# A four-layer graph network on one core: a selection matrix formed by transposes on PE, and table rows of 528 numbers

## The chip, the core and the metric

The kernel runs on one core of a Trainium2 chip. The metric is the device time of one execution in microseconds (us). PE is the matrix engine (PEld its weight loads), DVE the vector engine, ACT the scalar engine, POOL the general engine GpSimd, which here also issues the gathers, and SP the engine that issues the plain DMAs.

## The reference, cut to what matters

Eight batches of 2048 nodes with 64 features go through four layers over one sparse graph `adj`. Each layer normalizes its input, clamps it at zero, attends over a node's neighbours, and adds the result to its input.

```python
# layer 0: scores are dot products
h = jnp.maximum(_layernorm(x, axis=-1), 0.0)
x = x + _L0_gnn_ref(h, adj)
# layer 1: e[n,m] = leaky(s1[n] + s2[m]), then ELU
h = jnp.maximum(_layernorm(x, axis=-1), 0.0)
x = x + _L1_gnn_ref(h, adj, L1_gnn_W, L1_gnn_a)
# layer 2: four heads of dot products, a projection, then a second
# attention by dot products, then a layer norm
h = jnp.maximum(_layernorm(x, axis=-1), 0.0)
x = x + _L2_gnn_ref(h, adj, L2_gnn_Wh, ..., L2_gnn_beta)
# layer 3: like layer 1, with relu
h = jnp.maximum(_layernorm(x, axis=-1), 0.0)
x = x + _L3_gnn_ref(h, adj, L3_gnn_W, L3_gnn_a)
```

In the additive layers 1 and 3 a node needs of each neighbour its feature row (8 batches x 64 = 512 numbers) and the second term of its score, one number for each batch.

## The kernel before

**Tiles.** `edge_stack` cuts the 2048 nodes into 16 tiles of 128, one node for each partition, with all eight batches side by side (F = 512 numbers, B = 8 batches). Of the dense graph it makes lists of neighbours once. Tile i has `ROWS[i]` slots in which every node has one neighbour of its own, and `PACKED[i]` slots in which 128 further edges of any of the tile's nodes are packed: 81 slots in all, 32 of them packed (`sum(PACKED)`).

**Selection matrices.** For a packed slot, a 128x128 matrix of zeros and ones says which node an edge belongs to. `sel(i, t)` carries a node's value to its edges (`by_edge`, L406, and the query product in `scores`, L428); its transpose `selt(i, t)` sums edges back into their nodes (`by_query`, L392, and `weigh_sum`, L385). Both are made while the lists are made: `sel` by comparisons (L670), `selt` from it by transposes on PE and copies on ACT (L671 to L677). `selt_all` stays in the on-chip memory (SBUF) to the end. `sel_all[0]` lies in the pool `rows` (L582), which ends with layer 1; a copy of 2 MB goes to DRAM at L709, and is loaded back at L857, at the start of the stage after the heads.

**Stages.** In the order of the source: making of the lists and the first normalization; layer 0; layer 1 (`additive(1, ...)`, L710); the four heads of layer 2 (L714 to L849, pools `l2`, `ps_z`, `ps_s`, `ps_g`); the second attention of layer 2 (L852 to L902; the prediction calls it layer 3's start, after its table number 3); and the last layer (`additive(4, ...)`, L909, table 4; the prediction's layer 4). Each stage writes its rows to a table in DRAM (`store_rows`, L352), and the next gathers from it: one indirect DMA of 128 rows for each slot, issued by POOL (`gather`, L246), into a ring of 26 slots in SBUF (L100). So the first gather of a stage waits for the last row of the stage before.

**Tables.** Tables 1 and 4, of the two additive layers, have rows of F + B = 520 numbers: 512 features and, behind them, the 8 second terms, which `pre_d` copies there (L348). The others have 512. The ring has rows of 520 for all. The second terms are read as `g[:, :, F:]` (L507, L532, L535).

**Order.** Within a stage `pipeline` (L214) writes the tiles' steps in a skewed order: while one tile is gathered, the one before is scored, the one before that is weighted. In the second attention these are `take3` (gathers and the load of the tile's own rows), `first3` (squares L866, products L422 and L430, weights L436), `second3` (sums of weights, then `weigh_sum`: POOL multiplies rows by weights at L380, PE sums them at L385), `third3` and `fourth3`. That is not yet the order of the engines: the program is built with a planner that simulates the instructions' times and sorts each engine's queue by them:

```python
with tile.TileContext(nc, schedule_with_timeline_sim=True) as tc:
```

Buffers of a closed pool are handed on to the next one. The pools of the stage after the heads, where `sel` is to lie, and its sums in PSUM, are:

```python
with psum_pools()[0] as ps_q, psum_pools()[1] as ps_t, tc.tile_pool(name="rows2", bufs=2) as rp:
    ...
    sel_all[0] = rp.tile([P, sum(PACKED) * P], F32, name="sel", bufs=1)
    nc.sync.dma_start(out=sel_all[0], in_=sel_dram[:, :])
```

`ps_q` has three banks of 512 numbers.

Of the kernel before, what the change touches and what calls it, by code (L numbers as in the profile page):

```python
# [8 lines left out]
F32 = mybir.dt.float32  # L9
# [3 lines left out]
AF = mybir.ActivationFunctionType  # L13
OP = mybir.AluOpType
AX = mybir.AxisListType

P = 128
# [42 lines left out]
def edge_stack(ctx: ExitStack, tc: tile.TileContext, x_in, adj, w1, w1t, a1, wh, wht, bh, wo, bo,  # L60
# [9 lines left out]
    nc = tc.nc  # L70
    N, F = x_in.shape
    D = gamma.shape[0]
    B = F // D
# [22 lines left out]
    f1s = const.tile([P, NT, B], F32, name="f1s")  # L96
    over = const.tile([P, NT, 3], F32, name="over")
    most = const.tile([P, 5, NT], F32, name="most")
    least = const.tile([P, 2, NT], F32, name="least")
    ring = const.tile([P, RING, F + B], F32, name="g")  # L100
    qidx = const.tile([P, sum(PACKED)], I32, name="qidx")
    selt_all = const.tile([P, sum(PACKED), P], F32, name="selt")
# [3 lines left out]

    table = [tc.dram_tile([N + 2, F + B if k in (1, 4) else F], F32, name=f"table{k}")
             for k in range(5)]

    QW = B * H * D + B * H  # L110
    qtab = tc.dram_tile([N + 2, QW], F32, name="qtab")
    sel_dram = tc.dram_tile([P, sum(PACKED) * P], F32, name="seld")
    xs = [tc.dram_tile([P, F], F32, name=f"xs{i}") for i in range(NT)]
# [13 lines left out]
    nc.gpsimd.memset(zcol, 0.0)  # L127
    zrow = const.tile([1, F + B], F32, name="zrow")
    nc.gpsimd.memset(zrow[:, :F], 0.0)
# [104 lines left out]
    def rows(i, lo, hi, most=RING):  # L234

        t = lo
        while t < hi:
# [3 lines left out]
            t += m  # L241

    def row(i, t):
        return ring[:, (held[i] + t) % RING, :F]
# [68 lines left out]
    def pre_c(u):  # L313
        def f(i, st):
            st["xh"] = rows_pool[0].tile([P, F + B], F32, name="xh", bufs=3)
# [22 lines left out]
    def pre_d(k, u):  # L338

        def f(i, st):  # L340
            xh = st["xh"]
            if u is not None:
                p = ps_m.tile([P, F], F32, name="m")
                for j in range(F // P):
                    nc.tensor.matmul(p[:, 4 * j:4 * j + 4], st["xt"][:, j, :], u, start=True, stop=True)
                pv = p[:, :2 * B].rearrange("p (b t) -> p t b", t=2)
                nc.scalar.copy(f1s[:, i, :], pv[:, 0, :])
                nc.scalar.copy(xh[:, F:], pv[:, 1, :])  # L348
            store_rows(k, i, xh, k != 2)
        return f  # L350

    def store_rows(k, i, xh, mean):  # L352
        cols = table[k].shape[1]
        nc.sync.dma_start(out=table[k][i * P:(i + 1) * P, :], in_=xh[:, :cols])
        if mean:
            if i == order[0]:
                nc.gpsimd.tensor_copy(acc, xh[:, :F])
            else:
                nc.gpsimd.tensor_tensor(acc, acc, xh[:, :F], op=OP.add)
            if i == order[-1]:  # L360
                p = ps_m.tile([P, F], F32, name="m")
                nc.tensor.matmul(p[:1, :], ones, acc, start=True, stop=True)
                mr = rows_pool[0].tile([1, F + B], F32, name="mr", bufs=1)
                nc.vector.memset(mr[:, F:], 0.0)
                nc.vector.tensor_copy(mr[:, :F], p[:1, :])
                nc.sync.dma_start(out=table[k][N:N + 1, :], in_=mr[:, :cols])
# [133 lines left out]
    def additive(k, wd, *finish):  # L500
# [21 lines left out]
        def first(i, st):  # L522
# [57 lines left out]
    with tc.tile_pool(name="rows", bufs=2) as rp:  # L580
# [133 lines left out]
    with tc.tile_pool(name="l2", bufs=2) as l2p, \  # L714
# [116 lines left out]
        def fourth2(i, st):  # L831
# [9 lines left out]
            for b in range(4):  # L841
                nc.tensor.transpose(p[:, b * P:(b + 1) * P], ht[:, b * P:(b + 1) * P], ident)
            h2 = rows_pool[0].tile([P, F + B], F32, name="xh", bufs=3)
            nc.scalar.copy(h2[:, :F].rearrange("p (j b d) -> p b j d", j=2, d=D),
# [7 lines left out]
    with psum_pools()[0] as ps_q, psum_pools()[1] as ps_t, tc.tile_pool(name="rows2", bufs=2) as rp:  # L852
# [3 lines left out]
        sel_all[0] = rp.tile([P, sum(PACKED) * P], F32, name="sel", bufs=1)  # L856
        nc.sync.dma_start(out=sel_all[0], in_=sel_dram[:, :])  # L857

# [581 lines left out]
```

## Time and profile before

| what | value |
|---|---|
| median of three runs | 1717.97 us (1717.35 to 1723.83) |
| the profiled execution | 1721.51 us, span 1719.7 us |
| DMA in all | 266.94 MB in 85787 packets |
| of it gathers (POOL's queue) | 141.05 MB |
| plain DMAs (SP's queue) | 124.79 MB |
| gathers `g<-table,idx` | 405, POOL busy 986 ns with each |
| store and load of the selection matrix | 1 each, 2048 KB |

The stages by the profile's table of stretches (busy us of each engine, and share of the DMA engines in use):

| stretch, us | PE | DVE | ACT | POOL | DMA |
|---|---|---|---|---|---|
| 110 to 365, lists and layer 0 | 168.9 | 243.3 | 81.0 | 189.3 | 0.54 |
| 365 to 655, layer 1 | 214.4 | 202.7 | 157.2 | 132.6 | 0.54 |
| 655 to 1195, the heads | 470.2 | 430.5 | 258.4 | 459.1 | 0.45 |
| 1195 to 1262, passage to the second attention | 34.3 | 26.1 | 18.6 | 31.9 | 0.56 |
| 1262 to 1530, second attention | 185.5 | 227.6 | 135.1 | 196.1 | 0.34 |
| 1530 to 1720, last layer | 135.7 | 102.7 | 17.9 | 75.9 | 0.50 |

Times in the text are from the span's start. A line of the chain of waits reads: start, duration, then the engine or DMA that the end of the program was waiting on at that time. In a line of waits, "DVE mr L364 <- DMA table<-xh: 5.6, 1, 5.6" means that DVE, before the instruction of line 364 that writes `mr`, waited 5.6 us in all, once, 5.6 at most, and that the landing of that DMA ended the wait. "issue" is waiting that the profile explains by nothing, "remote" waiting ended by an event that it can't place.

### The profile page before, as it was taken

The numbers are of one execution on the slowest core, as the hardware profiler recorded it, in microseconds if no ns is written. First come the engines' busy times: TensorE is split into PE (matmuls) and PEld (weight loads), VectorE is DVE, ScalarE is ACT, GpSimd is POOL, SyncE is SP. The second block draws the span as 40 slices with busy tenths as digits, with TensorE's granted clock in tenths as the row PEclk, the third lists the DMA queues.
The fourth block names the chain that finished last, engine by engine and source line by source line (L and its number), as shares of the span: only waits on it lengthen the run. The fifth ranks groups of instructions, "written<-read, shape, count | busy, mean of one in ns | idle before, by whom it ended". The sixth has DMA issues, their size and how long they took to land.

```text
span 1719.7 us, 15784 instructions
## 1 busy us (share of the span) xinstructions
PE 1215.1 (71%) x3771; PEld 606.6 (35%) x3771; DVE 1318.4 (77%) x2748; ACT 744.5 (43%) x2378; POOL 1153.4 (67%) x903
## 2 busy tenths in 40 slices
PE   0025667776479974599997999999467877555877
PEld 0002334443234431234342444443223433333545
DVE  6979999992469987699997899831389889823656
ACT  5841324441146783356531545545234445620011
POOL 5766867786554125898789889985577896654540
PEclk9998876896699997799999999999787879657989
DMA  5555454455566447656255345200643542235651
GB/s 172 167 182 179 152 200 153 141 198 156 147 201 235 158 179 260 233 189 208 87 201 200 113 157 177 87 13 19 255 141 99 154 146 70 81 119 164 197 170 51
DMA packets 85787, 266.94 MB, mean 155 GB/s; under 512 B 14627, under 2 KB 14659, under 8 KB 75446
## 3 DMA queue, kind: packets, MB, share of 16 engines
q0 software_dynamic: 37328, 141.05, 26.7%
q1 hardware_dynamic: 48358, 124.79, 20.4%
q8 instruction: 32, 0.52, 0.1%
q14 instruction: 69, 0.57, 0.1%
HBM read 208.74 MB, written 57.05 MB: 155 GB/s over the span
## 4 chain that ended last, share of the span: by engine, by line
PE 25%; POOL 11%; DVE 9%; issue 7%; ACT 5%; DMA 3%; another core or an unknown queue 2%; DVEq 0%; SPq 0%; POOLq 0%; ACTq 0%
PE y L787 10%; PE y L385 4%; POOL g L253 3%; POOL wh L772 3%; PE m L836 2%; ACT yn L795 2%; PE m L824 2%; PE y L779 2%; POOL wg L380 1%; DMA g<-table,idx 1%; POOL ln_r L290 1%; DMA rows<-table 1%; PE m L399 1%; DVE prod L755 1%
## 5 line engine op out<-in xcount | busy, mean ns | idle before, releaser
L253 POOL DMA_INDIRECT g<-table,idx x405 | 399.2, 986 | 233.5 <-issue 161.7
L772 POOL TENSOR_TENSOR wh<-g,w 128x1024 f32<-128x1024 f32 x162 | 307.5, 1918 | 30.0 <-PE y L787 28.0
L385 PE MATMUL y<-wg,ident 128*128 128x512 f32 x392 | 234.5, 729 | 72.7 <-POOL wg L380 64.3
L290 POOL TENSOR_TENSOR ln_r<-ln_q,mhalf 128x8 f32<-128x8 f32 x80 | 135.8, 1701 | 160.6 <-DVE ln_q L288 85.1
L759 DVE TENSOR_REDUCE s<-prod 128x32 f32<-128x2048 f32 x81 | 184.0, 2286 | 14.8 <-ACT w L761 12.9
L380 POOL TENSOR_TENSOR wg<-g,w 128x1024 f32<-128x1024 f32 (+1 forms) x91 | 158.9, 1756 | 37.3 <-ACT w L436 24.2
L787 PE MATMUL y<-wh,ident 128*128 128x512 f32 x320 | 154.6, 610 | 28.9 <-POOL wh L785 25.1
L385 PE MATMUL y<-wg,selt 128*128 128x512 f32 x256 | 141.6, 663 | 5.4 <-POOL wg L380 4.4
L385 PEld LDWEIGHTS y<-wg,ident 128*128 128x128 f32 x392 | 81.6, 228 | 162.2 <-POOL wg L380 78.9
L787 PE MATMUL y<-wh,selt 128*128 128x512 f32 x256 | 124.7, 614 | 10.4 <-POOL wh L772 10.4
L795 ACT ACTIVATE yn<-y,rec 128x64 f32<-128x64 f32 x512 | 111.2, 368 | 27.5 <-PE y L787 26.9
L755 DVE TENSOR_TENSOR prod<-q,g 128x2048 f32<-128x2048 f32 x49 | 111.5, 2276 | 5.3 <-ACT g L753 4.6
L399 PE MATMUL m<-w,selt 128*128 128x8 f32 (+1 forms) x384 | 59.5, 258 | 76.0 <-ACT w L542 38.2
L380 DVE TENSOR_TENSOR wg<-g,tiny 128x1024 f32<-128x1024 f32 (+1 forms) x92 | 98.2, 1086 | 17.1 <-PE y L385 8.8
L399 PEld LDWEIGHTS m<-w,selt 128*128 128x128 f32 x384 | 63.5, 213 | 122.3 <-ACT w L542 43.6
L442 DVE SCALAR_TENSOR_TENSOR zt<-m,bhc,att 128x512 f32<-128x512 f32 x64 | 47.3, 738 | 75.0 <-ACT att L441 74.4
L298 ACT ACTIVATE xh<-x,ln_r 128x64 f32<-128x64 f32 x256 | 88.3, 428 | 18.8 <-POOL ln_r L292 18.7
L787 PEld LDWEIGHTS y<-wh,ident 128*128 128x128 f32 x320 | 59.0, 193 | 104.9 <-issue 63.8
L428 PE MATMUL q<-rows,sel 128*128 128x512 f32 x128 | 84.3, 762 | 15.7 <-DVE prod L422 5.0
L753 ACT COPY g<-g 128x512 f32<-128x512 f32 x81 | 50.4, 622 | 100.5 <-DVE prod L755 87.9
L755 DVE TENSOR_TENSOR prod<-qe,g 128x2048 f32<-128x2048 f32 x32 | 73.0, 2282 | 17.0 <-DMA qe<-qtab,qidx 15.9
L779 PE MATMUL y<-rows,ident 128*128 128x512 f32 x128 | 70.0, 634 | 18.3 <-DMA rows<-table 13.6
(210 smaller groups left out, 2584.7 us busy)
## 6 DMA issues: line engine op xcount, KB each, us to landing
qtab<-q SPq DMA_DIRECT2D x16, 1040.0 KB
a<-in_adj_dram SPq DMA_DIRECT2D x16, 1024.0 KB
q<-qtab SPq DMA_DIRECT2D x14, 1040.0 KB
table<-xh SPq DMA_DIRECT2D x48, 256.0 KB
rows<-table SPq DMA_DIRECT2D x48, 256.0 KB
xs<-x SPq DMA_DIRECT2D x48, 256.0 KB
x<-xs SPq DMA_DIRECT2D x48, 256.0 KB
table<-xh SPq DMA_DIRECT2D x32, 260.0 KB
```

Of the source, the lines that this page charges most:

```text
L253: nc.gpsimd.indirect_dma_start(out=ring[:, (held[i] + t) % RING, :cols], out_offset=None, in_=table[k][:, :], in_offset=bass.IndirectOffse ...
L290: nc.gpsimd.tensor_tensor(st["rstd"][:, 0, :], q, mhalf, op=OP.pow)
L298: nc.scalar.activation(dst[:, b * D:(b + 1) * D], st["src"][:, b * D:(b + 1) * D], func, bias=0.0 if st["less"] is None else r[:, 1, b:b + ...
L380: eng.tensor_tensor(wg[:, :m].rearrange("p t (b d) -> p t b d", b=B), g[:, :, :F].rearrange("p t (b d) -> p t b d", b=B), w[:, t0:t0 + m, ...
L385: nc.tensor.matmul(y, lhs(i, t), wg[:, t - t0, :], start=(t == 0 and own is None), stop=(t == n - 1))
L399: nc.tensor.matmul(p[:, :cols], selt(i, t), packed[:, t, :], start=(t == 0), stop=(t == T - 1))
L755: nc.vector.tensor_tensor(pr.rearrange("p (b h) d -> p b h d", h=H), q[:, :B * H * D].rearrange("p (b h d) -> p b h d", h=H, d=D), heads(g ...
L759: nc.vector.tensor_reduce(s[:, t - lo, :], pr, AX.X, OP.add)
L772: nc.gpsimd.tensor_tensor(wg, heads(row(i, t))[:, :, None, :].to_broadcast([P, B, 2, D]), w[:, :, 2 * k:2 * k + 2, None].to_broadcast([P, ...
L779: nc.tensor.matmul(st["ys"][j], ident, xb[:, 4 * j:4 * j + 4], start=True, stop=False)
L787: nc.tensor.matmul(st["ys"][j], lhs(i, t), wg[:, 4 * j:4 * j + 4], start=False, stop=(t == n - 1))
L795: nc.scalar.activation(yn[:, b, h, :], st["ys"][j][:, b, h, :], AF.Copy, scale=st["rec"][:, 4 * j + b, 2 * k + h:2 * k + h + 1])
```

## The change

Two things are changed. First, `sel` is no longer kept in DRAM across the heads: the store at L709, the load at L857 and the DRAM tensor go. At the place of the load, `selt_all` is transposed back on PE, four 128x128 blocks to a bank of `ps_q`, and ACT copies each bank into the new `sel` tile. Second, rows of tables 1 and 4, and of the ring, get F + 2B = 528 numbers: `pre_d` copies first and second terms as they lie in PSUM, in pairs, and the readers pick every second number behind the features.

```diff
-    ring = const.tile([P, RING, F + B], F32, name="g")
+    ring = const.tile([P, RING, F + 2 * B], F32, name="g")
...
-    table = [tc.dram_tile([N + 2, F + B if k in (1, 4) else F], F32, name=f"table{k}")
+    table = [tc.dram_tile([N + 2, F + 2 * B if k in (1, 4) else F], F32, name=f"table{k}")
...
-    sel_dram = tc.dram_tile([P, sum(PACKED) * P], F32, name="seld")
...
+    def second_terms(g):
+
+        return g[:, :, F:].rearrange("p t (b u) -> p t u b", u=2)[:, :, 1, :]
...
-                pv = p[:, :2 * B].rearrange("p (b t) -> p t b", t=2)
-                nc.scalar.copy(f1s[:, i, :], pv[:, 0, :])
-                nc.scalar.copy(xh[:, F:], pv[:, 1, :])
+                nc.scalar.copy(f1s[:, i, :], p[:, :2 * B].rearrange("p (b t) -> p t b", t=2)[:, 0, :])
+                nc.scalar.copy(xh[:, F:], p[:, :2 * B])
...
-                nc.scalar.activation(w[:, t:t + m], g[:, :, F:], AF.Exp, scale=1.0 / TEMP)
+                nc.scalar.activation(w[:, t:t + m], second_terms(g), AF.Exp, scale=1.0 / TEMP)
...
-                nc.vector.tensor_tensor(s[:, t:t + m, :], g[:, :, F:], pr[:, None, :B].to_broadcast([P, m, B]),
+                nc.vector.tensor_tensor(s[:, t:t + m, :], second_terms(g), pr[:, None, :B].to_broadcast([P, m, B]),
                                         op=OP.add)
...
-                nc.vector.tensor_tensor(s[:, t:t + m, :], g[:, :, F:], pv[:, t - K:t - K + m, :B], op=OP.add)
+                nc.vector.tensor_tensor(s[:, t:t + m, :], second_terms(g), pv[:, t - K:t - K + m, :B], op=OP.add)
...
-            nc.sync.dma_start(out=sel_dram[:, :], in_=sel_all[0])
...
-        nc.sync.dma_start(out=sel_all[0], in_=sel_dram[:, :])
+        for t0 in range(0, sum(PACKED), 4):
+            n = min(4, sum(PACKED) - t0)
+            p = ps_q.tile([P, F], F32, name="q")
+            for t in range(t0, t0 + n):
+                nc.tensor.transpose(p[:, (t - t0) * P:(t - t0 + 1) * P], selt_all[:, t, :], ident)
+            nc.scalar.copy(sel_all[0][:, t0 * P:(t0 + n) * P], p[:, :n * P])
```

The tiles `zrow`, `xh`, `mr` and `h2` get 528 numbers as well.

More of the change, by code (lines that the diff above doesn't have):

```diff
@@ L1 @@
-from contextlib import ExitStack
+from contextlib import ExitStack, nullcontext
 import concourse.bass as bass
@@ L127, in edge_stack @@
     nc.gpsimd.memset(zcol, 0.0)
-    zrow = const.tile([1, F + B], F32, name="zrow")
+    zrow = const.tile([1, F + 2 * B], F32, name="zrow")
     nc.gpsimd.memset(zrow[:, :F], 0.0)
@@ L314, in f @@
         def f(i, st):
-            st["xh"] = rows_pool[0].tile([P, F + B], F32, name="xh", bufs=3)
+            st["xh"] = rows_pool[0].tile([P, F + 2 * B], F32, name="xh", bufs=3)
             scaled(st["xh"], st, AF.Relu)
@@ L362, in store_rows @@
                 nc.tensor.matmul(p[:1, :], ones, acc, start=True, stop=True)
-                mr = rows_pool[0].tile([1, F + B], F32, name="mr", bufs=1)
+                mr = rows_pool[0].tile([1, F + 2 * B], F32, name="mr", bufs=1)
                 nc.vector.memset(mr[:, F:], 0.0)
@@ L842, in fourth2 @@
                 nc.tensor.transpose(p[:, b * P:(b + 1) * P], ht[:, b * P:(b + 1) * P], ident)
-            h2 = rows_pool[0].tile([P, F + B], F32, name="xh", bufs=3)
+            h2 = rows_pool[0].tile([P, F + 2 * B], F32, name="xh", bufs=3)
             nc.scalar.copy(h2[:, :F].rearrange("p (j b d) -> p b j d", j=2, d=D),
```

## The prediction

> **What bounds the kernel now.** No engine is full over the whole span, so I went from the page (shares by engine) to the stretches by layer, then to the chain of waits and to the table of short stretches around the start of layer 3, where the change works, and last to the waits of layers 1 and 4, where its longer rows work.
>
> ```profile
> span 1719.7 us, 15784 instructions
> PE 1215.1 (71%) x3771; PEld 606.6 (35%) x3771; DVE 1318.4 (77%) x2748; ACT 744.5 (43%) x2378; POOL 1153.4 (67%) x903
> 1195.00:1262.00 67.00, 34.25 (x96) 15.82 (x96) 26.14 (x51) 18.61 (x43) 31.88 (x32) 0.75 0.56 203
> 1262.00:1530.00 268.00, 185.48 (x534) 96.58 (x534) 227.59 (x464) 135.13 (x449) 196.05 (x145) 0.78 0.34 108
> ```
>
> The stretch 1195 to 1262 us is the passage from layer 2 to layer 3: no engine is busy for more than half of it. Then layer 3 runs with VectorE (DVE, third figure) at 227.6 of 268 us, 85%: it is bound by VectorE, so a lead won at its start is largely kept.
>
> The chain of waits through this passage:
>
> ```profile
> 1214.74 0.59 ACT xh L844
> 1215.35 1.99 DMA table<-xh
> 1217.61 0.32 SPq L857
> 1218.45 12.02 DMA rows<-table
> 1230.49 0.63 ACT sq L866
> ```
>
> The last rows of layer 2 are stored (1.99 us to landing), SyncE issues the load of the selection matrix (L857, 2 MB), and the first row loads of layer 3, issued behind it, need 12.02 us. The table of stretches says why (us, busy PE, PEld, DVE, ACT, POOL, granted clock, DMA share, GB/s):
>
> ```profile
> 1216.00:1218.00 2.00, 0.00 (x0) 0.00 (x0) 0.07 (x1) 0.00 (x0) 0.00 (x0) 0.51 0.35 131
> 1220.00:1222.00 2.00, 0.00 (x0) 0.00 (x0) 0.00 (x0) 0.00 (x0) 1.57 (x2) 0.50 0.98 410
> 1226.00:1228.00 2.00, 0.00 (x0) 0.00 (x0) 0.00 (x0) 0.00 (x0) 1.70 (x2) 0.50 1.04 364
> 1232.00:1236.00 4.00, 2.70 (x7) 1.15 (x5) 3.17 (x4) 1.26 (x2) 2.87 (x4) 0.86 1.03 389
> 1236.00:1244.00 8.00, 3.01 (x9) 2.08 (x10) 5.67 (x16) 2.14 (x6) 6.17 (x7) 0.75 1.04 388
> ```
>
> From 1220 to 1244 the DMA engines are full at some 390 GB/s, and until 1228 PE, DVE and ACT do nothing. PE's clock stands at 0.50 there.
>
> Three more lines, of waits in this passage, in layer 1 and in layer 4:
>
> ```profile
> DVE mr L364 <- DMA table<-xh: 5.6, 1, 5.6
> ACT e L570 <- remote: 44.4, 2, 29.5
> DVE x L906 <- remote: 13.3, 1, 13.3
> ```
>
> The first is the first write into the buffers of layer 3, a memset that depends on no data; it still waits until the last store out of layer 2's buffers has landed (1217.8). The new pool is not free before. The other two stand beside long rows of gathers on GpSimd (POOL) and come back below.
>
> [...] packets of 4160 bytes (two rows of 2080) have a median of 161 ns, of 4096 bytes 159. [...] In 390 to 402 us, where PE is busy 8.86 of 12 us with transposes and very small matmuls, the granted clock is 0.50[...].
>
> **The change, part by part.**
>
> *Removed at layer 3's start.* The issue at L857 (0.37 us from 1217.61 to the next issue) and 2.10 MB of transfer: at 390 GB/s 5.4 us of full DMA engines. Row loads then land about as fast as the store before them, 2 us: about 1220, not 1228.6.
>
> *Added there.* 32 transposes in 8 groups of four and 8 copies on ScalarE (ACT). A 128x512 copy out of PSUM takes 0.59 us (L844): 4.7 us in all. Four transposes take 0.66 us at full clock (L842) and 1.91 at half (L306 at 1505.38). The copies write into the new pool, so by the memset's wait none starts before 1217.8. The three PSUM banks of ps_q are free since about 1146 (last use of layer 2's sums), so three groups can be made earlier, behind the heads; the other five wait for a bank. At half clock: 1217.8 + 0.6 + 5 x 1.91 + 0.6 = 1228.6, the very moment at which ACT's first square (L866) starts now, and that square is queued behind the copies. Bounds: at full clock the copies decide, 1217.8 + 8 x 0.59 + 0.6 = 1223.1; with no group made earlier, 1217.8 + 8 x 1.91 + 0.6 = 1233.7. I take 1228.6, because PE has idled since 1214.7 and the clock fell at once. So the first tile gains nothing, within -5.5 and +5.1 us.
>
> *What comes next.* Now the five squares are strung out from 1228.62 to 1238.60, each waiting for its rows. With rows already there they need about 1.1 us each (square and copy). DVE, which they feed, is busy 10.6 of the 16 us from 1228 to 1244 and idle 5.4: the same 5.4 as the transfer. Late next is POOL, which issues 26 gathers in a row (1218.36 to 1250.69, one per 1.25 us) before its first product (L380); the weights for this would now be ready in time. The first matmul of y starts at 1256.71, held up by a DVE wait of 4.08 us at 1250.67; without it, it starts at about 1252.6. Gain between 4.1 and 5.4; taken 5.
>
> *The three early groups* cost PE 3 x 0.6 = 1.8 us in layer 2's tail, where it waits for ACT between steps (34.3 of 67 us busy). I charge 0.5, bounds 0 and 1.8.
>
> *The store at L709* (2 MB, 362 to 371 us) goes. DMA share is 0.87 to 1.06 meanwhile, but DVE is busy 2.00 of 2.00 us in most of it and waits once for a gather, 0.7 us: gain 0, at most 0.7. SyncE's issues behind it move up 0.4 us and nobody waits for them.
>
> *Rows of 528 numbers.* 162 gathers of 128 rows carry 32 bytes more: 0.66 MB. A gather is issued every 1.25 us, 270 kB each, 216 GB/s; the engines carry 390, so POOL's issue still sets the pace: 0, at most 0.66 MB / 390 GB/s = 1.7 us. ScalarE's copy (L348, 0.17 us x32) writes 16 numbers, not 8, from a plain source: 0. DVE and ACT read every second number (L532, L535, L507, 89 instructions of 0.16 to 0.23 us): the copy L347 with such a stride takes 0.17, a plain one of the same size, L519, 0.20, so 0; at most a tenth, 1.5 us.
>
> *Sum:* -5 + 0.5 = -4.5. The profiled execution took 1721.5 (span 1719.7 and 1.8 around it), so 1717.0; the median of the runs, 1718.0, is 3.5 lower: 1713.
>
> **The rivals.** All instructions are sorted per engine at build time by simulated times (line 1436; POOL's 26 gathers ahead of the first product are its work, the source order lets three tiles in). Another load and longer rows change these times, so the order from layer 1 on may differ.
>
> *A, as above:* 1713, own range 1705 to 1719. Chance 0.36.
>
> *B, hidden anyway:* the selection matrix at 1233.7, POOL's order as it is. For it: PE's clock of 0.50. Against it: ps_q was free 70 us earlier. 1718. Chance 0.12.
>
> *C, faster:* the planner, seeing the weights earlier, puts the first product ahead of some ten of the 26 gathers. For it: those weights are ready at 1239.6, 11 us before POOL takes them. Against: gathers have no wait and fill every gap. 10 x 1.25 = 12.5 us on top of A: 1700. Chance 0.27.
>
> *D, slower:* one more stall behind a run of gathers. In layer 1 ACT stood 29.5 us at L570 while POOL issued 35 gathers (402.5 to 446.2), in layer 4 DVE 13.3 us at L906 behind 32 of them. If the new order lays one instruction for a late tile ahead of work for early ones, on DVE or ACT, it pays about the smaller: 1718 + 13.3 = 1731. It decides as soon as such a stall exceeds the 4.5 us won. For it: layers 1 and 4 have their table rows, and so their planned times, changed. Against: a new order can as well shed those stalls. Chance 0.25.
>
> **How the numbers follow.** About 0.5% (8.6 us) is what a measurement of this kernel can tell from no change. A lies mostly within it; four in ten of A fall below 1709.4. Faster: 0.27 + 0.36 x 0.42 = 0.42. Same: 0.12 + 0.36 x 0.58 = 0.33. Slower: 0.25. The range 1694 to 1734 takes in A with its unknown costs, C and D's middle; a tenth of the chance stays out at each end.
>
> **What would show it.** In the profile after: no rows<-table of 12 us on the chain at layer 3's start; eight copies of 128x512 on ACT from about 1217.8, transposes of 1.91 us per four, the square L866 at about 1228; the DMA share falling below 1 some 5 us sooner; first y of layer 3 about 4 us earlier; gathers in layers 1 and 4 still 1.25 us apart. I am wrong on the first tile if the copies start well before the last store lands or the transposes keep the full clock; on the whole if layers 1 or 4, at unchanged instruction times, change their length by more than 5 us: then the order, not the work, made the result.

## The result, and the profile after

The changed kernel takes 1735.15 us (median of 7 runs, 1727.71 to 1739.51); before takes 1720.37 on the same chip (7 runs, 1717.35 to 1728.82). The ratio is 1.0059, with an interval of 1.0031 to 1.0088: slower by 0.6%. The profiled execution took 1735.15 us, 13.6 more than that of before. The page's first lines:

```profile
span 1733.4 us, 15850 instructions
PE 1236.1 (71%) x3803; PEld 615.3 (35%) x3803; DVE 1318.5 (76%) x2748; ACT 747.6 (43%) x2386; POOL 1153.2 (67%) x903
```

DVE, which bounds the stage that was changed, has the same 1318 us of work as before; what has grown is waiting. To find where, I cut both traces at the first gather of the second attention, at the end of its first stretch (1262) and at the store of its mean row. Before:

```profile
1218.36:1262.00 43.64, 20.00 (x46) 10.23 (x46) 21.58 (x44) 8.64 (x20) 31.88 (x32) 0.64 0.83 300
1262.00:1526.89 264.89, 185.48 (x534) 96.58 (x534) 227.59 (x464) 135.13 (x449) 195.09 (x144) 0.78 0.35 109
1526.89:1719.70 192.81, 135.70 (x547) 83.75 (x547) 102.71 (x372) 17.92 (x63) 76.90 (x81) 0.83 0.50 148
```

After:

```profile
1218.93:1262.00 43.07, 20.48 (x58) 11.89 (x58) 20.72 (x43) 11.78 (x27) 30.48 (x31) 0.62 0.75 256
1262.00:1539.71 277.71, 201.67 (x542) 99.78 (x542) 228.81 (x464) 134.48 (x450) 196.52 (x144) 0.76 0.33 104
1539.71:1733.40 193.69, 137.70 (x547) 86.00 (x547) 102.86 (x372) 17.58 (x63) 76.87 (x81) 0.81 0.50 149
```

The second attention took 308.5 us (43.64 + 264.89) and takes 320.8: +12.3. All before it is 0.6 us longer, the last layer 0.9. In the stage DVE and POOL do the same work (DVE 249.2 and 249.5 us); ACT has 2.5 us more, for the copies. PE is busy 16.7 us longer, 4.1 of it with the transposes; its granted clock over the stage is 0.74, and was 0.76. What slower matmuls add to DVE's waits was not separated.

**The start is better than predicted.** ACT's order, where the copies into `sel` (L863) and the squares (L872, L866 before) stand:

```profile
1218.27 1.56 ACT L863 COPY sel<-q 128x512 f32<-128x512 f32 x3 [2.28 <-DMA table<-xh]
...
1221.39 1.15 ACT L872 ACTIVATE sq<-rows 128x512 f32<-128x512 f32 x2
...
1228.72 0.62 ACT L872 ACTIVATE sq<-rows 128x512 f32<-128x512 f32 x1
```

The copies wait for the last store out of the old buffers, as foreseen, but the planner put squares between them. The first square starts at 1221.39, not at 1228.6; the fifth (1228.72) starts when the first one did before. The first DVE work on a tile comes 3.1 us after the first gather, against 10.9.

**Then the lead goes.** DVE's waits in the changed kernel from 1218 to 1262 (what it waits for, us in all, times, longest; `c` stands twice, for waits with different endings):

```profile
DVE c L874 <- issue: 6.2, 2, 3.4
DVE c L874 <- remote: 5.9, 1, 5.9
DVE prod L432 <- remote: 4.8, 1, 4.8
DVE rec L887 <- remote: 3.5, 1, 3.5
```

and in before:

```profile
DVE c L868 <- issue: 13.2, 4, 11.4
DVE rec L881 <- remote: 4.1, 1, 4.1
```

So before has one wait that ends on "remote" in this stretch, of 4.1 us; after has three, of 14.2 us. They stand here in DVE's order:

```profile
1244.39 0.69 DVE L874 TENSOR_REDUCE c<-sq 128x8 f32<-128x512 f32 x1 [5.92 <-remote]
...
1249.92 0.69 DVE L432 TENSOR_TENSOR prod<-q,g 128x512 f32<-128x512 f32 x1 [4.77 <-remote]
...
1257.04 0.17 DVE L887 SCALAR_TENSOR_TENSOR rec<-m,w 128x8 f32<-128x8 f32 x1 [3.51 <-remote]
```

and PE's results that they wait for, here:

```profile
1235.01 1.00 PE L414 MATMUL m<-c,sel 128*128 128x8 f32 x4
1236.01 3.78 PE L430 MATMUL q<-rows,sel 128*128 128x512 f32 x4
...
1246.85 0.57 PE L401 MATMUL m<-w,selt 128*128 128x8 f32 x2
```

Read together: by the tiles and the order of PE's updates of its semaphore, `c` needs the `m` that ended at 1236.01 (it read the buffer that `c` is to fill), `prod` a `q` that ended at 1238.09, `rec` the `m` that ended at 1247.42. DVE goes on 8.4, 11.8 and 9.6 us later. The trace records updates of that semaphore at 1244.30, 1249.90 and 1257.01, right ahead of DVE's starts. I call these late results; what lies between a recorded end and its update the traces do not show. In the rest of the second attention no DVE wait is of this sort; here they are 14.2 us, 10.1 more than in before. Both kernels have them in layers 1 and 4 too, at the waits that the prediction showed among others (in the trace of before, `e` goes on at 451.10, 28.3 us after the recorded end of its matmul at 422.82).

POOL meanwhile, from its last gather ahead of the first product:

```profile
1246.55 0.95 POOL L256 DMA_INDIRECT g<-table,idx  x1 [0.30 <-issue]
1247.52 2.90 POOL L382 TENSOR_TENSOR wg<-g,w 128x1024 f32<-128x1024 f32 x2
...
1256.88 0.95 POOL L256 DMA_INDIRECT g<-table,idx  x1 [0.30 <-issue]
1266.54 2.90 POOL L382 TENSOR_TENSOR wg<-g,w 128x1024 f32<-128x1024 f32 x2 [8.71 <-PE y L387]
```

The first product starts 3.2 us earlier than before, after 23 gathers in place of 26; six more gathers follow where three did. POOL then stands 8.7 us, because PE's first `y` starts at 1262.63. In before it started at 1256.71:

```profile
1256.71 3.76 PE L385 MATMUL y<-wg,ident 128*128 128x512 f32 x4
```

and in the changed kernel:

```profile
1262.18 0.60 PE L401 MATMUL m<-w,selt 128*128 128x8 f32 x2 [1.27 <-ACT w L438]
1262.63 3.76 PE L387 MATMUL y<-wg,ident 128*128 128x512 f32 x4
...
1271.04 1.69 PE L379 MATMUL y<-rows,ident 128*128 128x512 f32 x2 [2.94 <-DVE z L447]
1272.52 1.91 PE L387 MATMUL y<-wg,ident 128*128 128x512 f32 x2
```

In PE's new order the `m` of the fourth tile stands ahead of the first tile's `y`; it waits for weights that DVE's waits have delayed, though the product for `y` was done at 1250.4. Likewise the third tile's own `y` (L379, waiting for `z`) stands ahead of the second tile's.

**After the first `y`** more is lost. Of DVE's waits from 1262 to 1540:

```profile
DVE prod L424 <- ACT q L421: 12.9, 4, 7.2
...
DVE y L467 <- PE y L387: 9.7, 4, 6.3
```

and of before's, from 1262 to 1527:

```profile
DVE y L465 <- PE y L385: 6.9, 5, 2.4
...
DVE prod L422 <- ACT q L419: 0.4, 1, 0.4
```

The wait for `y` grew little, that for the query `q` is new. ACT's order shows why:

```profile
1374.67 0.32 ACT L301 ACTIVATE q<-ln_xc,ln_r 128x64 f32<-128x64 f32 x1 [2.84 <-POOL ln_r L293]
1374.92 0.57 ACT L421 COPY q<-rows 128x512 f32<-128x512 f32 x1
```

The query copy at L421 needs only rows that had landed by 1351.28, when a square on the last of them began, but it is queued behind another tile's normalization (L301), which waits 2.84 us for POOL. DVE's product waits 7.16 us for it, until 1375.53.

In sums over the stage: DVE idles 28.5 us from the first gather to its work on the first `y` (before 22.1), and 42.7 after that (before 37.3): +6.4 and +5.4, with 0.4 more of work the 12.3. The +6.4 is 10.1 us more of late results, 7.8 us less until the first work on a tile, and 4.1 in others. This says where DVE stood idle in two single profiles; whether the late results or the new order made it so is what the runs are for.

### The profile page after: what moved, and what is told of

The parts are those of the page before. It is cut to its first block, busy times and chain, and to the rows that moved or that the text cites. A ratio compares the mean times of both kernels' runs of the same rounds, so it can differ in the third digit from the quotient of the medians.

```text
span 1733.4 us, 15850 instructions
## 1 busy us (share of the span) xinstructions
PE 1236.1 (71%) x3803; PEld 615.3 (35%) x3803; DVE 1318.5 (76%) x2748; ACT 747.6 (43%) x2386; POOL 1153.2 (67%) x903
## 3 DMA queue, kind: packets, MB, share of 16 engines
q1 hardware_dynamic: 48070, 120.73, 19.6%
## 5 line engine op out<-in xcount | busy, mean ns | idle before, releaser
L387 PE MATMUL y<-wg,ident 128*128 128x512 f32 x392 | 238.3, 739 | 67.9 <-POOL wg L382 57.8
L760 DVE TENSOR_REDUCE s<-prod 128x32 f32<-128x2048 f32 x81 | 184.0, 2287 | 14.7 <-ACT w L762 12.8
L788 PE MATMUL y<-wh,selt 128*128 128x512 f32 x256 | 126.6, 622 | 10.1 <-POOL wh L773 10.0
L382 DVE TENSOR_TENSOR wg<-g,tiny 128x1024 f32<-128x1024 f32 (+1 forms) x92 | 98.1, 1086 | 19.7 <-PE y L387 10.6
L301 ACT ACTIVATE xh<-x,ln_r 128x64 f32<-128x64 f32 x256 | 88.3, 427 | 17.5 <-POOL ln_r L295 15.0
L780 PE MATMUL y<-rows,ident 128*128 128x512 f32 x128 | 69.9, 632 | 20.2 <-issue 15.5
```

What stands on the lines that cost most here:

```text
L301: nc.scalar.activation(dst[:, b * D:(b + 1) * D], st["src"][:, b * D:(b + 1) * D], func, bias=0.0 if st["less"] is None else r[:, 1, b:b + ...
L382: eng.tensor_tensor(wg[:, :m].rearrange("p t (b d) -> p t b d", b=B), g[:, :, :F].rearrange("p t (b d) -> p t b d", b=B), w[:, t0:t0 + m, ...
L387: nc.tensor.matmul(y, lhs(i, t), wg[:, t - t0, :], start=(t == 0 and own is None), stop=(t == n - 1))
L760: nc.vector.tensor_reduce(s[:, t - lo, :], pr, AX.X, OP.add)
L788: nc.tensor.matmul(st["ys"][j], lhs(i, t), wg[:, 4 * j:4 * j + 4], start=False, stop=(t == n - 1))
```

## The experiments

Two theories. P: results of PE reach the other engines late while POOL issues a long unbroken run of gathers, and the change moves more of DVE's work into such a run. O: the planner's new order is worse by itself, whatever PE's results do. Ratios are to before on the same chip, with their intervals; seven chips were used, each for one group of runs. In the tables, "late" is DVE's waiting that ended on "remote" and "copy" its waiting for the query copy (waits over 0.5 us), both in the second attention; "idle" is DVE's idle time from the first gather to its work on the first `y`, and after it; all in us, from one profile of each kernel. By the same columns, on the first chip, before has 22.1, 37.3, 4.1 and 0, and the change 28.5, 42.7, 14.2 and 12.9.

### Each part alone, and the load by pieces

These four ran on a second chip (before 1726.91 us). `r1_transposes_only` is before with the transposes and rows of 520. `r2_rows528_only` is the changed kernel with the store and the load of `sel` put back:

```diff
+            nc.sync.dma_start(out=sel_dram[:, :], in_=sel_all[0])
...
-        for t0 in range(0, sum(PACKED), 4):
-            ...
-            nc.scalar.copy(sel_all[0][:, t0 * P:(t0 + n) * P], p[:, :n * P])
+        nc.sync.dma_start(out=sel_all[0], in_=sel_dram[:, :])
```

> The kernel before with the transposes and copies in place of the round trip; the table rows keep 520 numbers. Every engine's order of instructions is then that of the changed kernel. Theory P (PE's results reach DVE late while GpSimd issues a long run of gathers, and the change moves PE's work into that run) and theory O (the new order in the second attention costs the time): as slow as the changed kernel, 1730 to 1738 us, and its profile shows the same three DVE waits of 5.9, 4.8 and 3.5 us between 1238 and 1257. Theory R (the longer rows cost it): 1720, as before.

> The changed kernel with the round trip of the selection matrix through DRAM put back; the rows keep 528 numbers. The order of instructions is nearly that of the kernel before (2 of PE's 2222, 1 of GpSimd's 905 stand elsewhere). Theories P and O: 1720, within 3 us of before, since the longer rows took 0.6 us up to the second attention. Theory R: 1730 or more.

`r3_rows_late` was to take the lead away again: the changed kernel with a 2.1 MB copy from DRAM to DRAM ahead of the row loads (`nc.sync.dma_start(out=pad[:, :], in_=qtab[:252, :])`). `r4_sel_by_tile` gets the rows early without transposes: before, with `sel` loaded in 16 pieces, each behind the row load of its tile in `take3`:

```diff
-        nc.sync.dma_start(out=sel_all[0], in_=sel_dram[:, :])
...
+            lo, hi = POFF[i] * P, (POFF[i] + PACKED[i]) * P
+            nc.sync.dma_start(out=sel_all[0][:, lo:hi], in_=sel_dram[:, lo:hi])
```

> The changed kernel with one DMA of 2.1 MB from DRAM to DRAM (part of the query table, its copy is read by nobody) issued ahead of the row loads of layer 3: the row loads land as late as in the kernel before, 1228, and the transposes stay. Theory P: the work that PE's late results hold up starts some 8 us later and meets a shorter rest of the run of gathers; about 1724, and the DVE waits for PE between 1238 and 1260 sum to under 8 us. If the transposes themselves cost the time (half clock, one bank each): 1735 or more, as these stay and the loads are late on top. Theory O: between the two, by whatever order the planner makes.

> The kernel before, but the selection matrix is loaded in 16 pieces, each behind the row load of the tile that needs it: no transposes, 520 numbers, and early row loads as in the changed kernel (about 1221). Theory P in the form that the early start alone is the harm: 1728 to 1735, with DVE waits for PE of over 10 us in the first 40 us of the stage. If the harm needs the transposes on PE: 1712 to 1720, with waits for PE as before (4.1 us).

| kernel | ratio | idle to first y | after | late | copy |
|---|---|---|---|---|---|
| r1_transposes_only | 1.0056 (1.0035 to 1.0077) | 27.6 | 41.9 | 6.0 | 12.5 |
| r2_rows528_only | 1.0003 (0.9987 to 1.0019) | 24.0 | 34.2 | 1.3 | 1.7 |
| r3_rows_late | 1.0054 (1.0038 to 1.0071) | 28.1 | 42.6 | 13.1 | 13.3 |
| r4_sel_by_tile | 1.0004 (0.9986 to 1.0021) | 21.3 | 36.8 | 13.0 | 2.5 |

The first part of the change, transposes in place of the round trip, brings the whole loss, the longer rows nothing measurable. r1's order is exactly that of the changed kernel on PE, DVE and POOL, and its idle sums and its waits after the first `y` are those of the changed kernel:

```profile
DVE prod L421 <- ACT q L418: 12.5, 4, 7.2
...
DVE y L464 <- PE y L384: 9.5, 4, 6.1
```

The three waits of 5.9, 4.8 and 3.5 us did not come as expected: `c` waits 1.2 us and `prod` 4.8 on "remote", and the third stands under "issue", so that the column counts 6.0:

```profile
1248.80 0.37 PE L398 MATMUL m<-w,selt 128*128 128x8 f32 x2
...
1263.83 0.17 DVE L884 SCALAR_TENSOR_TENSOR rec<-m,w 128x8 f32<-128x8 f32 x1 [5.26 <-issue]
```

`rec` goes on 14.7 us after the recorded end of its `m` at 1249.17. It looks like a third late result, though the profile places no event at its end; so "late" is a lower bound.

r3 missed its aim: the copy depended on nothing of its stage, the planner moved it up to 624.78 us, and the rows weren't late. It tells only that the result repeats on another chip. r4 fits neither of its two forecasts and sets a limit to P: with 13.0 us of late results, and early rows as in the change, it is as fast as before. Late results can eat a lead; r4 does not show them putting a kernel behind before.

### The order alone

The changed kernel with rules on PE's order for the first five tiles, `y` ahead of later tiles' sums (`e1_pe_order`); the gathers of the fourth to sixth tile put behind the products of the tile three places ahead, so that POOL's first run is 14 gathers and not 23 (`e2_gathers_held`); the same two edits in before (`e4_pe_order_before`, `e3_gathers_held_before`). Each rule names an instruction behind which others are issued; no work is added. The first two parts of the diff are the rules for PE, the last is that for the gathers (`last_y` and `last_wg` hold a tile's last matmul of `y` and its last product):

```diff
+    def behind(marks, k, on):
+        return tc.issue_after(marks[k]) if on and k in marks else nullcontext()
...
-            d, p = by_query(i, w, B)
+            with behind(last_y, k - 3, k < 5):
+                d, p = by_query(i, w, B)
...
-            st["y"] = weigh_sum(i, st, w, st["rows"])
+            with behind(last_y, k - 1, k < 5):
+                st["y"] = weigh_sum(i, st, w, st["rows"])
...
-            gather(3, i, st)
+            k = order.index(i)
+            with behind(last_wg, k - 3, k < 6):
+                gather(3, i, st)
```

> The changed kernel with PE's order corrected by hand for the first five tiles of the second attention: the sum of a tile's weights (L401) stands behind the last y of the tile three places earlier, and a tile's first y (L379) behind the last y of the tile before it; nothing else is asked of the planner. GpSimd's first run stays at 23 gathers. Theory O (PE's new order costs it: one weights' sum ahead of the first y, 1.3 us, and the third tile's first y, which waits for a free bank, ahead of the second tile's products, 4.4 us): the second tile's y comes some 6 us earlier, ratio to the kernel before 1.000 to 1.003. Theory P (PE's results reach DVE late during GpSimd's run of gathers, and that costs it): the DVE waits for PE before 1260 stay at 8 to 14 us and the ratio at 1.005 to 1.006.

> The changed kernel with GpSimd's gathers of the fourth to sixth tile of the second attention placed behind the products of the tile three places earlier: the first run is 14 gathers, not 23. Theory P: with the run cut short PE's results arrive in time, the DVE waits for PE before 1260 sum to less than 4 us (14.2 in the changed kernel), the 8 us by which the changed kernel is ahead at the first scores are kept, and the ratio to the kernel before is 0.994 to 0.999. Theory O alone: PE's order is another one again; the waits for PE stay above 8 us and the ratio above 1.000.

> The same holding of gathers in the kernel before (no transposes, round trip kept). Theory P: its one DVE wait for PE there (4.1 us) goes, ratio 0.996 to 0.999. If long runs of gathers do no harm: 1.000 within 0.002, and the wait stays.

> The same two rules for PE's order in the kernel before, as a control: there the order is already so for the first tiles, and 94 of PE's 2222 instructions stand elsewhere for other reasons. Both theories: 1.000 within 0.002. A larger difference shows how much a mere shuffle of the later order is worth, and that much of any other result is then noise of the planner.

| kernel | ratio | idle to first y | after | late | copy |
|---|---|---|---|---|---|
| e1_pe_order | 1.0040 (1.0027 to 1.0054) | 15.5 | 45.3 | 0 | 4.6 |
| e2_gathers_held | 1.0006 (0.9991 to 1.0022) | 9.5 | 47.2 | 0 | 9.1 |
| e3_gathers_held_before | 1.0052 (1.0030 to 1.0073) | 18.4 | 34.8 | 0 | 8.8 |
| e4_pe_order_before | 1.0041 (1.0030 to 1.0053) | 18.9 | 36.8 | 0 | 6.9 |

e1, e3 and e4 missed every range that was given for them. e4 does the same work as before in another order (beside PE's 94 instructions, some of DVE's, ACT's and POOL's moved too) and costs 0.4%: an order alone can be worth that much here. That makes O possible, and it puts 0.4% of uncertainty on every kernel below that has an order of its own; it does not show that the change's order is what costs. e1 speaks against one form of O: with `y` ahead of later tiles' sums, DVE's work on the first `y` comes 36.0 us after the first gather, as it does in the change on a chip of this kind (c1 below, 1.0029), and the time is no better.

The held gathers gain only where the rows are early; in before they cost 0.5% (e3), and not by waiting. DVE idles 3.5 us less in e3 than in before on such a chip (c2 below) but is busy 10.8 us more. All of that is one small operation, the variance of the normalization (`ln_q`, L288). Its median time is 0.16 us, and at the worst place it is this:

```profile
1254.73 4.07 DVE L288 TENSOR_SCALAR ln_q<-ln_q 128x8 f32<-128x8 f32 x1
1254.99 3.77 POOL L385 TENSOR_TENSOR wg<-g,w 128x1024 f32<-128x1024 f32 x2
```

It ends with POOL's products, and each of its twelve instances of over 0.4 us in e3's second attention ends within 0.04 us after an operation of POOL. Over that stage it sums to 25.5 us in e3 and to 13.3 in c2. On the first chip it takes 13.8 in the change and 12.3 in before, so it is not what slows the change. An idle sum misses such a stretch.

But this chip brought something else: before took 1671.94 us on it, 48 us less than on the first, and beside its runs of gathers PE's results are not late: ACT's wait at `e` in layer 1, 44.4 us in before on the first chip, is 4.7 to 4.9 (e1 and e4). So P could not be tried there, and the next question was the chip.

### The change on such a chip

On another chip I ran the change again (`c1_change`), before against itself (`c2_before`) and e2's kernel (`c3_gathers_held`); on a third, r4's kernel (`d1_sel_by_tile`), it with the gathers held (`d2_sel_by_tile_held`), e2's again (`d3_gathers_held`), and the gathers of all 16 tiles held, `k < 16` in the diff above (`d4_held_all`).

> The changed kernel itself, unaltered. The last four kernels ran on a chip on which the kernel before takes 1672 us, not 1720, and on which no wait for PE's late results is to be seen, in any layer. Theory P: the loss belongs to chips with late results; on a chip without them the ratio is 0.996 to 1.001, as the 8 us of lead at the first scores are kept there. Theory O (order): the new order costs on every chip, ratio 1.004 to 1.007. On a chip with late results both give 1.005 to 1.006 again.

> The kernel before, unaltered, for its profile on the same chip as the other two: ratio 1.000. On a chip without late results its stage from the first gather of the second attention to the store of the mean row should be shorter than 308.5 us by about the one wait of 4.1 us, and layers 1 and 4 shorter by their waits of 44 and 13 us.

> The changed kernel with the gathers of the fourth to sixth tile held (as in e2). On a chip with late results theory P: ratio 0.992 to 0.999, because the three waits of 14.2 us shrink; theory O: 1.000, as it was on the other chip. On a chip without late results: 1.000 again for both.

> The kernel before with the selection matrix loaded by tile (as in r4, where a wait of 13.0 us for a late PE result ate a lead of 9 us: ratio 1.0004). On a chip without late results: the lead is there at the first y, and what remains of it at the end tells what the order after it costs; theory P 0.995 to 0.999, theory O 1.000 to 1.003. On a chip with late results: 1.000 again.

> As d1, and the gathers of the fourth to sixth tile of the second attention stand behind the products of the tile three places earlier (first run 14 gathers, not 22). On a chip with late results theory P: the 13.0 us wait shrinks below 5, ratio 0.993 to 0.998. Theory O: 1.000 to 1.004, whatever the waits do. On a chip without late results: as d1 within 0.002.

> The changed kernel with the gathers held, once more (as e2, c3). On a chip with late results theory P: the three waits of 14.2 us shrink below 5 and the ratio is 0.996 to 1.001, against 1.0059 of the changed kernel. If the waits shrink and the ratio stays above 1.004, the waits were not what cost the time. On a chip without late results: 1.001.

> The changed kernel with every tile's gathers placed behind the products of the tile three places earlier, for all 16 tiles: the first run is 9 gathers. Both theories: no wait for late results in the first 40 us, and the first y some 20 us earlier than in the changed kernel. If the stage is bound by DVE's work, the lead stays and the ratio is 0.988 to 0.995; if later order gives it back, 1.000 or more.

| kernel | ratio | idle to first y | after | late | copy |
|---|---|---|---|---|---|
| c1_change | 1.0029 (1.0017 to 1.0040) | 15.5 | 44.8 | 0 | 14.3 |
| c2_before | 1.0005 (0.9994 to 1.0016) | 18.0 | 38.7 | 0 | 0.5 |
| c3_gathers_held | 1.0017 (1.0001 to 1.0032) | 9.6 | 46.0 | 0 | 10.6 |
| d1_sel_by_tile | 1.0020 (1.0008 to 1.0033) | 13.1 | 42.2 | 0 | 2.5 |
| d2_sel_by_tile_held | 0.9992 (0.9977 to 1.0007) | 8.0 | 41.9 | 0 | 5.9 |
| d3_gathers_held | 0.9997 (0.9984 to 1.0010) | 9.1 | 43.6 | 0 | 9.7 |
| d4_held_all | 1.0023 (1.0014 to 1.0033) | 7.3 | 50.3 | 0 | 4.1 |

I call the chips on which results are late the first kind, the others the second. Both of these are of the second kind: before takes 1673.15 and 1672.52 us, and the waits at `e` in layer 1 of before (c2) are down to

```profile
ACT e L570 <- PE q L561: 6.0, 6, 2.1
```

c2's second attention takes 306.7 us, 1.8 less than on the first chip where 4.1 was expected; its layer 1 is 21.2 us shorter and its last layer 27.5, not 44 and 13.

There the change still costs 0.29%, about half as much, and without one late result. That lies between the ranges of P (to 1.001) and of O (from 1.004): neither alone foresaw it. DVE's waits of the change from 1200 to 1262 (its first gather is at 1198.95):

```profile
DVE y L467 <- PE y L387: 10.5, 3, 8.2
DVE c L874 <- ACT sq L872: 5.5, 3, 3.4
```

and of before on the same chip:

```profile
DVE c L868 <- ACT sq L866: 15.4, 5, 11.3
DVE y L465 <- PE y L385: 5.5, 2, 3.0
```

The lead in the scores is there (`c` waits 5.5 us for its squares, not 15.4), and it is spent at once: DVE then stands at the first `y` for up to 8.2 us, because POOL takes 23 gathers ahead of the first product. PE's first `y` still comes 3.8 us sooner after the first gather than in c2 (30.5 us, not 34.3), which is about the gain that was predicted; after it DVE idles 6.1 us more than in before. So it goes, more or less, with every version that has a lead: up to the first `y`, e2, c3 and d4 idle 8 to 11 us less than c2, and behind it 7 to 12 us more; d2 and d3 9 to 10 us less, and then 3 to 5 more. In the two profiles c1 is 8.1 us longer than c2: 3.0 in the second attention, 3.9 in the last layer and 1.2 before. So on this kind of chip a good part of the loss may lie in the last layer; these are single profiles, and c1's is 1.4 us above its median, c2's 1.1 below.

Holding the gathers helps here too, with no late results to shorten: d2 is 0.28% below d1, where the same ratio within 0.002 was expected.

### The gathers held where results are late

`f1_gathers_held` is e2's kernel, `f2_sel_by_tile_held` is d2's, on another chip of the first kind (before 1724.27 us).

> The changed kernel with the gathers of the fourth to sixth tile held (as e2, c3, d3). On a chip with late results theory P: the three waits of 14.2 us shrink below 5 and the ratio is 0.996 to 1.001, against 1.0059 of the changed kernel. If the waits shrink and the ratio stays above 1.004, the waits were not what cost the time there. On a chip without late results: 1.0005 again, within 0.0015.

> The kernel before with the selection matrix loaded by tile and the gathers held (as d2). On a chip with late results theory P: the wait of 13.0 us that r4 had there shrinks below 5, ratio 0.993 to 0.998, better than both kernels. On a chip without late results: 0.999 again, within 0.0015.

f1: 0.9986 (0.9972 to 1.0000); f2: 0.9970 (0.9954 to 0.9985), which beats both kernels. f1's DVE waits from 1218 to 1262:

```profile
DVE c L881 <- ACT sq L879: 3.8, 2, 3.1
```

Beside the wait of its opening memset for the last store, and one of 2.7 us for "issue", the others there are below 2 us, and no "remote" is left; DVE idles 8.9 us to the first `y`, not 28.5; its work on the first `y` comes 24.5 us after the first gather (49.2 in the change). After it, it idles 48.5, not 42.7, so of 19.6 us some 6 go again. On the same chip layers 1 and 4, which were not touched, still have their late results (f2's ACT 45.2 us, see below). So on this kind of chip a shorter run gains 0.7% on the change (1.0059 to 0.9986), on the other 0.1 to 0.3% (1.0029 to 1.0017 and 0.9997). These are the same two programs on both kinds, so their orders are the same, and the difference, some 0.4 to 0.6% with an uncertainty nearly as large, is P's share. The other pair of programs does not repeat it: `sel` by tile gains 0.34% from the held gathers here (r4 1.0004 to f2 0.9970), and 0.28% where no result is late (d1 1.0020 to d2 0.9992), although 13.0 us of late results went only here. With these intervals its share for P is anything from nothing to some 0.4%. So P is supported for the change by one pair, not by both.

### The run of gathers, or the gathers

Holding gathers back changed both the run and the traffic in it. `g1_pauses` is f2's kernel with the 35 and 32 gathers that open layers 1 and 4 left as they are, but two small POOL operations after every tenth:

```diff
+            if k in (1, 4) and issued[k] % 10 == 0:
+                with tc.issue_after(g.ins):
+                    for _ in range(2):
+                        pause[0] = nc.gpsimd.tensor_tensor(rest, rest, mhalf, op=OP.pow).ins
```

> f2's kernel, and in layers 1 and 4 two small POOL operations after every 10 gathers, so that the runs of 35 and 32 gathers are cut into runs of 10 at most; the pauses add work on POOL (some 55 us of it in all by the durations of POOL's small operations). Theory P (results of PE reach the other engines late while POOL issues an unbroken run of more than about 14 gathers, on some chips): on a chip where before shows the waits of 29.5 + 15 us in layer 1 and 13 us in layer 4, these vanish, and the time is 0.975 to 0.985 of before less what POOL's own work costs. On a chip where before shows no such waits nothing is won: 1.000 to 1.006 of before. Rival (it is the number of gathers in flight or their traffic that delays, not the unbroken run): the waits stay, 10 us or more each, on a chip that has them in before, and the ratio is 1.000 or more.

Measured, again on a chip of the first kind (before 1725.72 us): 1708.79 us, 0.9910 (0.9879 to 0.9941), the lowest ratio of all versions. (The execution that was profiled, 1698.65 us, is the shortest of its five; the others took 1708.42 to 1710.74.) In f2 ACT's waits at `e` in layer 1, and DVE's at `x` in layer 4, were:

```profile
ACT e L575 <- remote: 45.2, 2, 30.2
...
DVE x L915 <- remote: 13.3, 1, 13.3
```

In g1 the longest such wait, in the whole trace, is:

```profile
ACT e L586 <- remote: 8.0, 1, 8.0
```

What ends on "remote" sums to 17 us on DVE and ACT in g1, to 72 in f2. The wait above ends at 436.85, two us into a pause:

```profile
433.85 0.95 POOL L258 DMA_INDIRECT g<-table,idx  x1 [0.30 <-issue]
434.83 3.38 POOL L265 TENSOR_TENSOR rest<-rest,mhalf 128x8 f32<-128x8 f32 x2
```

Over the first 44 us of layer 1's gathers, f2 (403.34 to 446.85) and g1 (406.56 to 450.76), columns as in the stretches:

```profile
403.34:446.85 43.51, 14.42 (x48) 7.81 (x48) 10.42 (x41) 1.25 (x4) 33.16 (x35) 0.66 0.73 204
```

```profile
406.56:450.76 44.20, 28.18 (x106) 16.95 (x107) 25.72 (x86) 9.15 (x29) 35.42 (x34) 0.73 0.63 183
```

The traffic is 183 GB/s in place of 204, a tenth less, and PE does twice the work. With a pause of 3.4 us after ten gathers, what had stood for 30 us stands for 8 at most: this points to the unbroken run, more than to the traffic. Not excluded are a threshold in the traffic between these two rates, and that it is POOL's work of another kind, rather than the pause, that lets the results through. From its first gather to the next stage's, layer 1 takes 246.8 us (f2: 257.5), and the last layer, to the end, 174.6 (187.3). The pauses gave the planner a new order as well, and f2 and g1 ran on two chips, so of the 0.6% between them not all need be the late results'. The pauses cost 52.9 us of POOL, and I had expected 0.975 to 0.985 before that cost: the late waits went, but most of what they had taken was not won.

## Why the prediction was wrong

Predicted: 1713 us, 1694 to 1734; measured 1735.15. By its steps:

- *Row loads of 12 us go; rows land about 1220*: right, the first square on them is at 1221.39.
- *Eight copies not before 1217.8, five groups at half clock, first square at 1228.6*: the copies yes (1218.27). The groups were cheaper: twelve transposes, three groups, in 2.82 us, 0.94 each, not 1.91, at the same granted clock of 0.50. That the clock would stay at half for all five was the author's estimate: the last two groups, at a mean of 0.82, took 0.63 us each. The 1.91 was one reading, after 10 us in which PE had idled; at 393.91 of the same trace, also at 0.50, four take 1.43. And the square was not queued behind the copies. The first tile gained 7.2 us, where "nothing, within -5.5 and +5.1" was said.
- *Squares no longer strung out*: right.
- *POOL is late next; without the wait of 4.08 us the first `y` starts at 1252.6; gain 5*: **this step failed.** The wait was treated as a matter of its own place, which an earlier start would remove. It was one sample of late results, of which layers 1 and 4 of the same trace show larger ones. The earlier start put three waits of DVE into the run of gathers in place of one, 14.2 us; and the first `y` came at 1262.63, not at 1252.6. (Where no result is late it came about as much sooner as forecast, 3.8 us, and the change still lost 0.29%: there the next step alone failed.)
- *A lead won at the start is largely kept, since DVE is 85% busy*: failed too. f1 and c3 won 13.2 us (of 22.1) and 8.4 (of 18.0) up to the first `y` and then idled 11.2 and 7.3 us more than before. A busy share of 85% does not say that a lead is kept; what DVE waits for in the other 15% has to be followed too.
- *Three early groups cost 0.5*: layers 0 to 2 are 0.6 longer. *The store 0, the rows of 528 numbers 0*: r2 1.0003; gathers still 1.25 us apart with 0.67 MB more; strided reads at L534 and L537 take the 170 and 160 ns that L532 and L535 took.
- *Wrong on the whole if layers 1 or 4 change by 5 us*: on this chip they don't (at most 0.9 for layer 4). The loss here lies in the second attention.

The rival D had the kind of loss (a stall behind a run of gathers, an instruction for a late tile ahead of an early one's work) and its size (13.3 us; the medians differ by 14.8). The size is luck: it is made up of three late waits, a gain at the start and a loss after the first `y`, not of one stall of 13.3. It named the longer rows as the reason for a new order, and there it was wrong: r2 clears them. I gave it 0.25, although before's own page showed three stalls of its kind and no reason why an earlier start should escape them.

How the loss splits: 0.29% without late results, 0.59% with them; the intervals overlap, so "half each" is rough, and that late results are the second half rests on f1. What makes the first half, and which of the moved instructions costs the 5 to 6 us of idling after the first `y`, was not isolated; the query copy on ACT is the largest new wait on both kinds of chip, but e4 and d1 lose 0.2 to 0.4% with less of it. PE's order ahead of the first `y` is not it, as far as e1 shows. Why PE's results stand still during the run, and why on some chips only, stays open. Keeping `sel` in SBUF to the end, which would need neither load nor transposes, was not tried.

## What to carry to other kernels

A wait that ends on no event the profile can place is a sign to look at what else runs at that time, everywhere on the page, before a gain is counted on its removal: here 4.1 us of it became 14.2. A step that lets work start earlier must be followed to the next resource that serves it (here POOL's run of gathers, then PE's order): a lead is worth what is left after that, not what it is at the start. With a planner, an edit is also a new draw of the order, worth 0.4% here at equal work, and a gain below that needs the same program on both sides of a comparison. Here, breaking up a long run of gathers went with a faster program where late waits showed behind it (the change 1.0059, f1 0.9986; f2 0.9970, g1 0.9910); without an early start it cost 0.5% (e3).

## What had not been expected of the hardware

- PE's results reached DVE and ACT 8.4 to 11.8 us after their recorded ends at the three waits of the change, 14.7 us in r1, and in layer 1 28.3 us in before and 29.0 in the change (421.13 to 450.13), with 10 to 16 gathers in the 20 us ahead of such waits in the traces of these two. They come through in bunches: in before's trace four updates of PE's semaphore, long due, arrive within 0.17 us from 451.07. In layer 1 of before it begins some 17 us into the run of 35 gathers, which starts at 402.51 (ACT takes at 421.03 what ended at 419.62); with runs of 14 (f1, f2) there was none in the second attention.
- It goes with the chip: on three chips (before 1672 to 1673 us) this was not seen in any trace's layer 1, on four (1720 to 1727 us) in each trace. The last layer of before takes 165.3 us on one of the three, 192.8 on one of the four. Each chip was used at one time only, so chip and time are not told apart.
- Pauses of 3.4 us on POOL, doing useless work, went with a faster program: 0.9970 for f2, 0.9910 with the pauses, on two chips of the same kind.
- A DVE operation of 0.16 us took up to 4.07 us beside POOL's products and ended with them (e3), which counts as busy time and not as a wait.
- Transposes at one granted clock, 0.50, took 0.94 us per four in a run of twelve (the change, 1218.90), and 1.43 and 1.91 us elsewhere (before, 393.91 and 1505.38).
